# A four-layer image network on one core: the third layer's first pass issued in program order, the fourth layer's first inputs on three engines, and the first layer's gates placed between its transpositions

## The chip, the cores and the metric

The kernel runs on 1 core of one Trainium2 chip. The metric is the device time of one execution in microseconds. Engines are named as in the profile: PE (TensorE, matrix products and transpositions), PEld (its weight loads), DVE (VectorE), ACT (ScalarE), POOL (GpSimd) and SP (SyncE, which issues most DMAs). All data is 32-bit floating point.

## The reference

Eight images of 56 x 56 pixels and 192 channels go through four layers; each is a group normalization (32 groups), an operation, and a residual addition.

```python
x = x + L0(gn(x)); x = x + L1(gn(x)); x = x + L2(gn(x)); x = x + L3(gn(x))

# L0: gated Toeplitz operator, D1 = 576
p, q, v = silu(x @ p_w.T + p_b), silu(x @ q_w.T + q_b), silu(x @ v_w.T + v_b)
qv = q * v
o1 = toeplitz along w of qv with a1;  o2 = toeplitz along h of qv with a2
out = (p * (o1 + o2)) @ o_w.T + o_b

# L2: windowed attention over 8 x 8 windows, E = 384, S = 128
u, v, base = split(silu(x @ W_uv + b_uv))
lk = rope over the image(base * lk_g + lk_b)
lin_kv = sum over all tokens of lk^T (v / tokens)      # needs every token first
attn = relu(qq @ qk^T / 64 + bias) ** 2
out = u * (attn @ v + lq @ lin_kv) @ W_proj + b_proj

# L3: linear recurrences along four directions
h_t = h_{t-1} @ A + Bv * x_t;  y_t = Cv * h_t + (Dv + res) * x_t   # rows, columns, two diagonals
```

L1 (an attention over 3 x 3 patches) isn't touched.

## The kernel before, in words

The four layers run one after the other in one program. A framework places tiles in pools, inserts all semaphores, and orders the instructions of each engine by a plan made ahead of the run. Where a block is entered with `tc.manual_schedule(engines=...)`, the instructions of those engines keep the order in which the code states them, among those of that block; instructions of engines that aren't named, and of other blocks, may be placed by the plan wherever it thinks them ready.

**First layer (`layer0`, L136).** PE is in program order (L627); the other engines aren't. Each image goes through `NC = 5` chunks of channels, `c` = 0 to 4; chunks 0 to 3 have 128 channels, the last 64. For a chunk: `project` (L283) makes q and v from the normalized image in four steps `g` (PE products into accumulators from `banks()`, four in all, each of two PSUM banks; then two Silus on ACT into tiles `s`, of which there are four; then `multiply`, on DVE and POOL, writes the products into the one tile `qv`). Then `turn_both` (L342; `turn` for the last chunk) transposes `qv` in seven steps: 16 transpositions on PE into one accumulator, and two copies out of it, one on DVE and one on ACT (L357). Then `convolve` (L382) multiplies by the Toeplitz matrices. After chunks 1 and 3, `post` gates and projects back. The main loop (L634) interleaves lists of steps with `merge`: the transpositions of chunk `c` with the list `fill` (`post` or `post_tail` of an earlier chunk; `fill` is empty at c = 1 and c = 3 and at the very first chunk), then `project` of the next chunk with `beside` (statistics and normalization), then the convolutions; at `c == NC - 2` the steps of `project` and of `convolve` alternate.

**Third layer (`layer2`, L1241), first pass.** Its pools lie partly where the second layer's tiles lay. 52 iterations `n` (L1497) run over 50 groups of two tiles of 128 tokens, for pairs of images. In iteration `n`, PE multiplies the normalized tokens by `wvb` (`project`, L1412, accumulators `v`: three), `gates` (L1423) adds the bias on DVE (`sm`) and takes the Silu on ACT (`vb`), `keys` (L1433) stores v and builds the rotated key `l1` on POOL and DVE from the tables `ta`, `tb`, `tn`; two iterations later PE transposes the group's base (`turn`, into the one accumulator `t`) and adds `l1^T v` to `kv` (`sum_up`). `key_tables(c)` (L1380) loads six tiles' worth of the cosine and sine tables and multiplies the gains in, on DVE and POOL; it is called for c = 0 ahead of the loop and for the other four at the start of n = 1, 4, 7 and 10. `fetch` loads a chunk of the image (a chunk is seven tiles; SP queue, the first one ACT queue), `ready` normalizes it (ACT, and DVE for the second image) into window order. At given iterations `jobs` (L1490) run: the last statistics of the second layer (n = 3, 5, 7; two of them use the accumulator `t`), and loads of the second pass's weights, tables and bias. Only PE is in program order here (L1347). The second pass (L1527) puts DVE, ACT and POOL in program order too, SP not.

**Fourth layer (`layer3`, L1815).** PE, DVE, ACT and POOL are in program order. For each of four pairs of images, `inputs` (L1882) makes `u = scale * y + offset` in three parts `j`, one instruction of 128 x 3136 elements each; `inputs_diagonal` copies the diagonals on POOL; `step` (L1906) runs the recurrence, with the states in `ringv` and `ringh`. The first pair's `y` is loaded near the end of the third layer into tiles that are kept for it. At the start, inputs 0 and 1 are made on ACT and input 2 on POOL (L1993). The pool `l3u` (L1845) holds `us[0]` and then the two rings, in memory in which the second pass's tiles (`xa`, `xb`, `vt` and others) lay; a tile waits for what used its place.

Of the kernel before, what the change touches and what calls it, by code (L numbers as in the profile page):

```python
# [135 lines left out]
def layer0(cx, xin, xout, w, consts):  # L136
# [14 lines left out]
    with ExitStack() as es:  # L151
# [130 lines left out]

        def project(xn, c):  # L283

            n = 7 * H
            tail = c == NC - 1
            js = [2 * c] if tail else [2 * c, 2 * c + 1]

            def step(g):
                pss = [banks() for _ in js]  # L290
                for j, ps in zip(js, pss):
                    for h in range(2):
                        at = h * HQ + g * n
                        nc.tensor.matmul(  # L294
                            ps[:, h, 0:n], wqv[0][:, j, :], xn[0][:, at : at + n],
                            start=True, stop=False,
                        )
                for j, ps in zip(js, pss):
                    for h in range(2):
                        rows = slice(h * CB, (h + 1) * CB)  # L300
                        nc.tensor.matmul(  # L301
                            ps[:, h, 0:n], wqv[1][rows, j, :], xn[1][rows, g * n : (g + 1) * n],
                            start=False, stop=True,
                        )
                ts = []
                for i in range(2):
                    j, ps = js[0 if tail else i], pss[0 if tail else i]
                    rows = slice(i * DS, (i + 1) * DS) if tail else slice(0, 128)
                    t = cx.tile(wk, [128, 2, n], "s")[0 : DS if tail else 128]
                    nc.scalar.activation(t, ps[rows, :, 0:n], AF.Silu, bias=bqv[rows, j : j + 1])  # L310
                    ts.append(t)
                multiply(g, slice(0, DS if tail else 128), ts)

            return [lambda g=g: step(g) for g in range(4)]

        def multiply(g, rows, ts):

# [311 lines left out]
        merge(normalize(xn), [])  # L629
        for n in range(2):  # L630
            toeplitz(n)
        merge(project(xn, 0), [])
        fill, after, telling = [], None, []
        for b in range(B):  # L634
            more = b + 1 < B
            for c in range(NC):
                n = b * NS + 2 * c
                two = c < NC - 1
                turns = turn_both(n) if two else turn(n)
                merge(fill, turns)  # L640
                fill, beside = [], []
                if c == 0:
                    if after is not None:
                        image_dma(nc.sync, xout[b - 1], *after, store=True)
                        beside, telling = tell(b - 1, *after)
                    if more:
                        nxt = load_raw(b + 1)
                if c == 1:
                    acc = new_acc(b)
                    beside = [lambda f=f: f(bank) for f in telling]  # L650
                if c == 2 and more:
                    beside = normalize(nxt)

                if c % 2 == 0:
                    ot = cx.tile(cp, [120, 128, H] if two else [H, H, DS], "ot")
                ahead = project(xn, c + 1) if two else project(nxt, 0) if more else []
                convs = []
                for m in (n, n + 1) if two else (n,):
                    *some, last = convolve(m, ot)
                    convs += some + [lambda m=m, last=last: (last(), toeplitz(m + 2))]  # L660

                if c == NC - 2:
                    ahead = [f for pair in zip(ahead, convs[0:4]) for f in pair]
                    convs = convs[4:]
                merge(ahead, beside)
                for f in convs:
                    f()
                if c in (1, 3):
                    fill = post(c // 2, xn, ot, acc)
            fill, after = post_tail(xn, ot, acc), acc  # L670
            xn = nxt
# [569 lines left out]
def layer2(cx, xin, xout, w, consts):  # L1241
# [15 lines left out]
    with ExitStack() as es:  # L1257
# [90 lines left out]


        with ExitStack() as ps1:  # L1350
            def pool(name, bufs, **kw):
                return ps1.enter_context(tc.tile_pool(name=name, bufs=bufs, reuse_waits="tile", **kw))

# [23 lines left out]
            TW = 6  # L1377
            chunks = [(p, c) for p in range(NPAIR) for c in range(4)]

            def key_tables(c):  # L1380
                at = slice(c * TW, min((c + 1) * TW, NCH))
                n = at.stop - at.start
                a, b, t = ta[:, at], tb[:, at], tn[:, at]
                nc.sync.dma_start(a, consts["cos_rows"][:, at])
                nc.scalar.dma_start(b, consts["sin_rows"][:, at])
                g = [gk[:, i, :].unsqueeze(1).to_broadcast([128, n, S]) for i in range(4)]
                tmp = cx.tile(c1, [128, TW, S], "tmp")[:, 0:n]
                nc.vector.tensor_tensor(t, a, g[2], ALU.mult)
                nc.gpsimd.tensor_tensor(tmp, b, g[3], ALU.mult)
                nc.vector.tensor_tensor(a, a, g[0], ALU.mult)  # L1390
                nc.gpsimd.tensor_tensor(b, b, g[1], ALU.mult)
                nc.vector.tensor_tensor(t, t, tmp, ALU.add)
# [90 lines left out]

            ready(0)
            nc.scalar.dma_start(gk, w["lk_gb"].partition_broadcast(128))
            key_tables(0)
            fetch(1)


            jobs = [(3 + 2 * k, f) for k, f in enumerate(cx.late)]  # L1490
# [5 lines left out]
            kept = {}  # L1496
            for n in range(len(groups) + 2):  # L1497
                pvs = []
                if n in (1, 4, 7, 10):
                    key_tables((n + 2) // 3)  # L1500
                for at, job in jobs:
                    if at == n:
                        job()
                if n < len(groups):
                    p, g, ns = groups[n]
                    c = 4 * p + min(g // CW, 3)
                    if c + 1 not in xws:
                        fetch(c + 2)
                        ready(c + 1)
                    pvs = [cx.tile(psv, [128, 2, 512], "v") for _ in range(ns)]  # L1510
                    vb = cx.tile(wk, [128, 2, 2, E + S], "vb", bufs=4)
                    project(p, g, 0, pvs[0])
# [4 lines left out]
                if n < len(groups):  # L1517
                    for s in range(1, ns):
                        project(p, g + s, 0, pvs[s])
                    for s in range(ns):  # L1520
                        project(p, g + s, 1, pvs[s])
                        gates(g + s, pvs[s], vb, s)
                    kept[n] = (groups[n], keys(p, g, ns, vb), vb)
            nc.vector.tensor_scalar(kv, pkv, 1.0 / HW, None, ALU.mult)

# [289 lines left out]
def layer3(cx, xin, xout, w, consts):  # L1815
# [17 lines left out]
    with ExitStack() as es:  # L1833
# [9 lines left out]
        ys = [over.y, [cx.tile(cp, [128, HW], f"y1{j}") for j in range(2)]]  # L1843
        sps = [pool("l3s0")]
        up = pool("l3u")  # L1845
        us = [cx.tile(up, [128, 3, NS, NS], "u0")]
        rings = [cx.tile(up, [128, NR, 3, NS], f"ring{k}") for k in "hv"]
        sps.append(pool("l3s1", 2))
        yp = pool("l3y")
        ys[1].append(cx.tile(yp, [128, HW], "y12"))  # L1850
# [139 lines left out]
        loaded = {}  # L1990
        coefficients(0, over.nn[0])
        for j in range(3):
            inputs((nc.scalar, nc.scalar, nc.gpsimd)[j], 0, j)  # L1993
        inputs_diagonal(0)
        loaded[1] = load(1)
        plans = {g: prepare(g) for g in range(1, NG)}
# [96 lines left out]
```

## Time and profile before

| | us |
|---|---|
| median of 3 runs | 4215.12 (4203.36 to 4217.38) |
| profiled execution, its own time | 4220.94 |
| its span, first to last instruction | 4219.1 |
| first layer | 0 to about 2060 |
| second layer | to about 2717 |
| third layer, first pass | to 3177 |
| third layer, second pass | to 3857 |
| fourth layer | to the end |
| PE busy | 3948.1 (94% of the span) |
| DVE, ACT, POOL busy | 2336.7, 1785.5, 1512.0 |

The mean clock granted to PE is 0.978 of full speed. In the lines below, a line of the timeline has its start, its length, the engine, the line of the kernel, the operation, its output and inputs with their shapes, how many instructions are merged in it, and in brackets the idle time before it and what ended it. Durations of PE are modelled in part, since its instructions overlap. In the first layer an image takes about 249 us, as the distance of like stretches shows.

### The profile page before, as it was taken

How to read it: one execution, taken by the hardware profiler on the slowest of the kernel's cores; microseconds unless marked ns; L12 is line 12 of the kernel's file. 1: busy time of each engine (PE TensorE's matmuls, PEld its weight loads, DVE VectorE, ACT ScalarE, POOL GpSimd, SP SyncE). 2: the span in 40 equal slices, each digit the busy share in tenths (PEclk: the TensorE clock that was granted, in tenths of full speed). 3: DMA queues.
4: the chain of work that ended last, by engine and by line, in shares of the span. 5: the costliest groups of instructions: out<-in, count | busy, mean ns of one | idle time of the engine just before them, and what ended most of it. 6: DMA issues, size and time to landing. Idle time of an engine off the chain costs nothing.

```text
span 4219.1 us, 106491 instructions
## 1 busy us (share of the span) xinstructions
PE 3948.1 (94%) x46380; PEld 2547.7 (60%) x46380; DVE 2336.7 (55%) x3407; ACT 1785.5 (42%) x2022; POOL 1512.0 (36%) x1302
## 2 busy tenths in 40 slices
PE   6989999999999999999799999799998999998997
PEld 4666656666665666656466666444444555555997
DVE  5536565554656546554544444465656667664664
ACT  2434434334443434444233344233335555554564
POOL 3222232222322222242233333333334444443776
PEclk9999999999999999999899999899999999999999
DMA  6755242242524224242324444565538776663233
GB/s 145 141 107 146 62 116 66 77 97 62 146 62 113 58 70 115 62 105 66 92 66 110 105 101 106 138 185 186 167 130 192 174 171 150 159 144 104 81 110 94
DMA packets 382342, 483.54 MB, mean 115 GB/s; under 512 B 176084, under 2 KB 326724, under 8 KB 380484
## 3 DMA queue, kind: packets, MB, share of 16 engines
q1 hardware_dynamic: 375029, 467.19, 44.0%
q10 hardware_dynamic: 6847, 9.54, 0.8%
q8 instruction: 365, 5.98, 0.6%
q14 instruction: 101, 0.83, 0.1%
HBM read 320.90 MB, written 155.65 MB: 113 GB/s over the span
## 4 chain that ended last, share of the span: by engine, by line
PE 76%; DVE 7%; issue 6%; DMA 3%; POOL 3%; ACT 3%; SPq 1%; ACTq 0%; POOLq 0%; DVEq 0%
PE c L294 9%; PE h L1926 7%; PE v L1418 6%; PE c L395 6%; PE c L301 5%; PE c L481 5%; PE c L436 4%; PE c L948 4%; PE c L461 3%; PE y L983 3%; PE kv L1478 3%; PE c L443 3%; PE c L486 2%; DVE ol L357 2%; PE c L954 2%
## 5 line engine op out<-in xcount | busy, mean ns | idle before, releaser
L325 POOL TENSOR_TENSOR qv<-s,s 128x392 f32<-128x392 f32 (+3 forms) x320 | 567.2, 1793 | 1423.4 <-ACT s L310 1382.5
L310 ACT ACTIVATE s<-c,bqv 128x784 f32<-128x784 f32 (+1 forms) x320 | 278.5, 911 | 383.8 <-PE c L301 224.0
L294 PE MATMUL c<-xa,wqv 128*128 128x392 f32 x1152 | 432.3, 517 | 9.3 <-ACT or L357 6.5
L319 DVE TENSOR_TENSOR qv<-s,s 128x784 f32<-128x784 f32 (+1 forms) x160 | 190.5, 1190 | 267.0 <-ACT s L310 266.9
L357 ACT COPY or<-c 56x1024 f32<-56x1024 f32 x224 | 225.9, 1008 | 256.2 <-DVE ol L357 241.2
L294 PEld LDWEIGHTS c<-xa,wqv 128*128 128x128 f32 x1152 | 210.5, 194 | 177.3 <-issue 42.5
L395 PEld LDWEIGHTS c<-or,ol 120*64 120x64 f32 x9216 | 278.1, 138 | 59.4 <-issue 49.5
L395 PE MATMUL c<-or,ol 120*64 120x56 f32 x9216 | 288.7, 223 | 21.5 <-issue 8.4
L357 DVE COPY ol<-c 56x1024 f32<-56x1024 f32 x224 | 261.6, 1210 | 64.1 <-PE c L352 64.1
L450 ACT ACTIVATE s<-c,bp 128x448 f32<-128x448 f32 x224 | 129.9, 631 | 269.9 <-PE c L443 269.9
L301 PE MATMUL c<-xb,wqv 64*128 64x392 f32 x1152 | 232.9, 518 | 0.0
L1418 PE MATMUL v<-wvb,wa 128*128 128x512 f32 (+1 forms) x400 | 192.9, 615 | 28.7 <-ACT wa L1307 16.8
L1957 POOL TENSOR_TENSOR y<-y,s 128x448 f32<-128x448 f32 x168 | 185.0, 1101 | 91.9 <-ACT s L1936 88.6
L1926 PE MATMUL h<-ringv,am 128*64 128x57 f32 (+1 forms) x4400 | 192.4, 235 | 24.0 <-DVE ringv L1913 17.1
L481 PE MATMUL c<-po,wo 128*128 128x448 f32 x448 | 198.1, 564 | 10.8 <-DVE po L470 10.8
L1429 ACT ACTIVATE vb<-sm 128x1024 f32<-128x1024 f32 (+1 forms) x100 | 103.9, 1040 | 222.2 <-issue 195.6
L436 PE MATMUL c<-xa,wp 128*128 128x224 f32 x896 | 191.3, 356 | 3.6 <-issue 3.6
L1926 PE MATMUL h<-ringh,am 128*64 128x57 f32 (+1 forms) x4400 | 186.5, 232 | 8.4 <-DVE ringh L1932 7.8
L424 DVE TENSOR_TENSOR acca<-c,acca 128x392 f32<-128x392 f32 (+1 forms) x120 | 67.3, 588 | 222.0 <-PE c L486 204.8
L352 PE MATMUL c<-ident,qv 64*120 64x64 f32 x3584 | 143.2, 226 | 44.4 <-ACT or L357 38.9
L1926 PEld LDWEIGHTS h<-ringv,am 128*64 128x64 f32 x4400 | 168.1, 140 | 27.2 <-DVE ringv L1913 18.0
L948 PE MATMUL c<-wv,xc 128*126 128x192 f32 x896 | 175.6, 339 | 0.2 <-ACT v L958 0.2
(230 smaller groups left out, 7681.8 us busy)
## 6 DMA issues: line engine op xcount, KB each, us to landing
or<-tt SPq DMA_DIRECT2D x252, 196.0 KB
ol<-tt SPq DMA_DIRECT2D x252, 196.0 KB
vt<-v SPq DMA_DIRECT2D x56, 672.0 KB
v<-vb SPq DMA_DIRECT2D x96, 384.0 KB
x<-x SPq DMA_DIRECT2D x110, 168.0 KB
x<-x SPq DMA_DIRECT2D x110, 112.0 KB
bs<-bt SPq DMA_DIRECT2D x48, 256.0 KB
bs<-bs SPq DMA_DIRECT2D x54, 224.0 KB
```

What stands on the lines that cost most here:

```text
L294: nc.tensor.matmul(ps[:, h, 0:n], wqv[0][:, j, :], xn[0][:, at : at + n], start=True, stop=False,)
L301: nc.tensor.matmul(ps[:, h, 0:n], wqv[1][rows, j, :], xn[1][rows, g * n : (g + 1) * n], start=False, stop=True,)
L310: nc.scalar.activation(t, ps[rows, :, 0:n], AF.Silu, bias=bqv[rows, j : j + 1])
L319: nc.vector.tensor_tensor(sub(qv[rows, 7 * g :, 64 + H - 1 :], (HH * 120, 2), (120, 7), (-1, H)), *(t.rearrange("p u (h w) -> p u h w", w= ...
L325: eng.tensor_tensor(sub(qv[rows, w0:, H - 1 - 7 * g - HH * u :], (120, w1 - w0), (-1, 7)), *(t[:, u].rearrange("p (h w) -> p w h", w=H)[:, ...
L357: copy(dst[:, :, :, i0 : i0 + 8], view[rows])
L395: nc.tensor.matmul(ps[u * 64 : (u + 1) * 64, k, v * H : (v + 1) * H], left[:, d * H : d * H + 64], right[:, d * H : (d + 1) * H], start=Tr ...
L436: nc.tensor.matmul(out(u, h), wp[0][:, 2 * j + u, :], xn[0][:, at : at + n], start=(u == 0), stop=True, skip_group_check=True,)
L481: nc.tensor.matmul(pa, wo[:, 2 * j + u, 0:CA], pos[u], start=(u == 0), stop=(u == 1))
L948: nc.tensor.matmul(out(i, u), group(i, u), wv[0], start=(u == 0), stop=True, skip_group_check=True,)
L1418: nc.tensor.matmul(out, x[:, at : at + n], wt, start=(k == 0), stop=(k == 1), skip_group_check=True,)
L1926: nc.tensor.matmul(ps[sides[c], y], am[a][:, m * CB : (m + 1) * CB], old[:, x], start=(n < 2), stop=True, skip_group_check=True,)
```

## The change

First layer: `project` returns, for each step, a pair of functions: `gates` (products and Silus) and `products` (`multiply`). `whole` joins them again. In the main loop, `project` of the next chunk is called ahead of the transpositions; where `fill` is empty, the first two steps' `gates` are merged with the transpositions and their `products` follow them; the other steps run whole, as before. At `c == NC - 2` only as many steps of `convolve` alternate as steps of `project` are left.

Third layer, first pass: DVE, ACT, POOL and SP are put in program order. The table loads move out of `key_tables` into `fetch_tables`, both on SP: tables 0 ahead of the loop and ahead of `fetch(1)`, tables 1 after it, the others at n = 1, 4 and 7. `key_tables(0)` moves into the loop, and all its calls from an iteration's start to between `gates` and `keys`. The second chunk's `ready` and third chunk's `fetch` move from n = 0 to n = 2.

Fourth layer: the rings are placed ahead of `us[0]`, and the first pair's input 1 is made on DVE.

```diff
@@ project @@
-            def step(g):
+            state = {}
+
+            def gates(g):
                 pss = [banks() for _ in js]
...
-                multiply(g, slice(0, DS if tail else 128), ts)
-
-            return [lambda g=g: step(g) for g in range(4)]
+                state[g] = ts
+
+            def products(g):
+                multiply(g, slice(0, DS if tail else 128), state.pop(g))
+
+            return [(lambda g=g: gates(g), lambda g=g: products(g)) for g in range(4)]
@@ layer0, main loop @@
-        merge(project(xn, 0), [])
+        def whole(steps):
+            return [lambda f=f, h=h: (f(), h()) for f, h in steps]
+
+        merge(whole(project(xn, 0)), [])
...
-                merge(fill, turns)
+
+                ahead = project(xn, c + 1) if two else project(nxt, 0) if more else []
+                early = [] if fill else ahead[0:2]
+                merge(fill + [f for f, _ in early], turns)
+                for _, f in early:
+                    f()
+                ahead = whole(ahead[len(early) :])
...
-                ahead = project(xn, c + 1) if two else project(nxt, 0) if more else []
...
                 if c == NC - 2:
-                    ahead = [f for pair in zip(ahead, convs[0:4]) for f in pair]
-                    convs = convs[4:]
+                    k = len(ahead)
+                    ahead = [f for pair in zip(ahead, convs[0:k]) for f in pair]
+                    convs = convs[k:]
@@ layer2, first pass @@
         with ExitStack() as ps1:
+            ps1.enter_context(
+                tc.manual_schedule(engines={ET.DVE, ET.Activation, ET.Pool, ET.SP})
+            )
...
+            def fetch_tables(c):
+                at = slice(c * TW, min((c + 1) * TW, NCH))
+                nc.sync.dma_start(ta[:, at], consts["cos_rows"][:, at])
+                nc.sync.dma_start(tb[:, at], consts["sin_rows"][:, at])
+
             def key_tables(c):
...
-                nc.sync.dma_start(a, consts["cos_rows"][:, at])
-                nc.scalar.dma_start(b, consts["sin_rows"][:, at])
...
             nc.scalar.dma_start(gk, w["lk_gb"].partition_broadcast(128))
-            key_tables(0)
+            fetch_tables(0)
             fetch(1)
+            fetch_tables(1)
...
-                if n in (1, 4, 7, 10):
-                    key_tables((n + 2) // 3)
...
-                    if c + 1 not in xws:
+                    if n >= 2 and c + 1 not in xws:
                         fetch(c + 2)
                         ready(c + 1)
...
                         gates(g + s, pvs[s], vb, s)
+                    if n in (0, 1, 4, 7, 10):
+                        key_tables((n + 2) // 3)
+                        if n in (1, 4, 7):
+                            fetch_tables((n + 5) // 3)
                     kept[n] = (groups[n], keys(p, g, ns, vb), vb)
@@ layer3 @@
         up = pool("l3u")
+        rings = [cx.tile(up, [128, NR, 3, NS], f"ring{k}") for k in "hv"]
         us = [cx.tile(up, [128, 3, NS, NS], "u0")]
-        rings = [cx.tile(up, [128, NR, 3, NS], f"ring{k}") for k in "hv"]
...
-            inputs((nc.scalar, nc.scalar, nc.gpsimd)[j], 0, j)
+            inputs((nc.scalar, nc.vector, nc.gpsimd)[j], 0, j)
```

## The prediction

> **What bounds the kernel now.** I read the page first (busy shares, the chain that ended last), then busy time by stretches with the granted clock, then the timeline at every place where the TensorE (PE) stands still, then DVE alone inside the third layer's first pass. The page's chain, by engine:
>
> ```profile
> PE 76%; DVE 7%; issue 6%; DMA 3%; POOL 3%; ACT 3%; SPq 1%; ACTq 0%; POOLq 0%; DVEq 0%
> ```
>
> PE sets the pace, busy 3948.1 of 4219.1 us. So only time in which PE waits or runs at half clock can be won, and the change aims at three such places. By stretches (start:end, length, busy us of PE, PEld, DVE, ACT, POOL, granted clock, DMA share, GB/s):
>
> ```profile
> 616.30:619.60 3.30, 2.88 (x7) 1.60 (x6) 2.73 (x3) 2.93 (x4) 0.00 (x0) 0.51 0.94 276
> ...
> 2722.00:2734.20 12.20, 0.00 (x0) 0.00 (x0) 8.81 (x12) 0.81 (x2) 10.86 (x4) 0.51 0.85 231
> 2734.20:2753.00 18.80, 6.92 (x8) 2.35 (x8) 14.11 (x14) 6.02 (x8) 11.51 (x7) 0.50 0.64 148
> ...
> 3857.20:3870.10 12.90, 0.00 (x0) 0.00 (x0) 2.05 (x4) 6.53 (x3) 6.25 (x6) 0.69 0.65 184
> 3870.10:3882.70 12.60, 10.75 (x158) 10.06 (x160) 3.70 (x14) 5.89 (x2) 7.02 (x13) 0.50 0.73 213
> ```
>
> See: PE does nothing in the second and fourth line, 0.37 of its time in the third, and each pause is followed by half clock. The 15.2 us pause at 3177 between the third layer's passes is not touched.
>
> First layer, transpositions with nothing between them (timeline):
>
> ```profile
> 363.61 6.87 DVE L357 COPY ol<-c 56x1024 f32<-56x1024 f32 x6 [0.21 <-PE c L352]
> ...
> 367.05 0.69 PE L352 MATMUL c<-ident,qv 64*120 64x64 f32 x16 [0.45 <-ACT or L357]
> ...
> 368.18 2.90 PE L294 MATMUL c<-xa,wqv 128*128 128x392 f32 x8 [0.44 <-ACT or L357]
> ```
>
> See: PE needs 0.69 us for a step, the copies 6.87/6 = 1.15 us, so PE waits for a free accumulator. L352 has 44.4 us of such idle time in the page's groups.
>
> Third layer's start:
>
> ```profile
> 2734.20 2.07 PE L1418 MATMUL v<-wvb,wa 128*128 128x512 f32 x2 [16.78 <-ACT wa L1307]
> ...
> 2748.15 5.17 PE L1418 MATMUL v<-wvb,wa 128*128 128x512 f32 x6 [11.88 <-DVE wa L49]
> ```
>
> See: 16.78 us until ACT's input, 11.88 more until DVE's half of it, because DVE first worked through the five key tables (the chain of waits for 2700 to 2760 runs through `tb`, `tmp`, `tn`, `ta`). Inside the pass, DVE alone:
>
> ```profile
> 2785.68 2.36 DVE L1428 TENSOR_TENSOR sm<-v,bvb 128x1024 f32<-128x1024 f32 x2 [1.41 <-PE v L1418]
> 2788.18 0.16 DVE L1176 COPY gms<-t 128x3 f32<-128x3 f32 x1
> ...
> 2792.15 0.69 DVE L1455 TENSOR_TENSOR l<-l,l 128x512 f32<-128x512 f32 x1 [1.16 <-POOL l L1448]
> ```
>
> See: DVE runs in the program's order already, with 1.41 us of slack per group of 8.57 us, save that `gms` went ahead of `l`.
>
> Fourth layer's start:
>
> ```profile
> 3862.79 5.89 ACT L1875 ACTIVATE u<-y,co 128x3136 f32<-128x3136 f32 x2 [4.93 <-DMA x<-xb]
> ...
> 3870.11 1.49 PE L1926 MATMUL h<-ringv,am 128*64 128x114 f32 x20 [12.94 <-DVE ringv L1913]
> ```
>
> See: ACT waits for the last stores of layer 2 (`u` lies where their tiles lay), then makes two of three inputs one after the other.
>
> [...] Here ACT's copies wait for DVE's (241.2 us at L357), though they read other partitions. [...] The trace moves 231 GB/s at a share of 0.85 between 2722 and 2734, so order matters there.
>
> **Part 1, first layer.** Where no post-processing fills the transpositions (c = 1 and 3 of eight images, and c = 0 of the first: 17 places) two of four gate steps now stand before and among them, their products after. Nothing is added. A full gate step is 4.34 us of PE (340.51 to 344.85), its two Silus 1.72. Before: 6.4 us (transpositions and wait) + 2 x 4.35 = 15.1 until the third gate step. After, from zero: gates 0 to 4.35; steps 0 to 2 to 5.95 (the third waits for gate 0's Silu); gates 1 from 6.15 to 10.5; steps 3 to 6 to 12.9 (the last wait for its Silu); the third gate step wants the accumulators of steps 3 and 4, which copies at 1.1 us free at 13.4: it starts at 13.5. Gain 1.6. At c = 3 the gate step has one half, 2.2 us of PE, and the copies are the longer: 0.6 to 1.6, I take 1.2. Sum 8 x 1.6 + 8 x 1.2 + 2 = 24.4. Half-clock stretches right after the bare turns (616, 978, 1227: clock 0.51, 0.51, 0.50, about 1.6 us lost each) should go: 4. The products now start on POOL only when the transpositions have read `qv`. Cover: 16 us of convolutions follow the gates, and POOL needs 4 us per step, ending at about 28 as before. The four `s` buffers are held by the early gates: the third Silu comes (19) after POOL's first product (17). The statistics' two small matmuls at c = 1 now have one gate step between them, 4.35 against a DVE chain of 3.4: at most 1 us in all. Part 1: -28, bounds -10 and -42.
>
> **Part 2, third layer's first pass.** First, the start. DVE, ACT, POOL and SP keep program order, so the input comes before the tables, and the last three of five table pairs (384, 384 and 64 KB each table: 1.7 of 3.2 MB) are no longer fetched ahead of it. The input's target tile overlaps layer 1's last strips; their last update ends on DVE at 2719.5, the stores go out to about 2722 and land 2 us later (before, stores queued among the tables until 2726.8). ACT and DVE each need 0.73 to 0.76 for the first piece: PE starts at 2726.5 (2725 to 2731), and is not stopped for DVE. The third matmul comes at 2728.6 instead of 2748.15: -19.6. Second, what the order gives back. (a) At group 5 the statistics' `gms` copy frees the only `t` bank. In order it stands behind group 4's `l`, and behind the tables of groups 0, 1 and 4 (three operations of 0.96 us, L1388 to L1392: 2.9 us of DVE each). With DVE caught up, as in the trace of before, it comes at 2792.9, and the transposition that needs the bank at 2789.8: 3.1 us. But the three table sets put DVE back by 1.8 each (1.1 lies in its wait for the Silu), and groups 0 and 1 have no sums for PE to do, so PE gains another 1.5 on DVE there, while slack gives back about 1: late by 6, a wait of 9. I take 9, and 2 for the half clock after it. (b) Square root at group 7 behind group 6's Silu: 0.7. (c) DVE late at groups 2 to 4: 0.5. (d) `gbs` at group 18 waits for its six DMAs, about 3 us, inside the slack of 4 to 5 that three accumulators give; SP's 8 bias rows per group (about 0.5 us each) fit 8.57. Later groups run the order they had, cost 0. Queued behind these waits: on DVE `sm`, for which PE waits only two groups later; on SP the v and bt stores, with four and two buffers. Part 2: -19.6 + 12.2 = -7.4, bounds -17 (3.1 instead of 11) and +5 (start at 2731, more waits at 12 to 13).
>
> **Part 3, fourth layer.** Rings come before `u0`, which by the tile sizes moves `u0` 21.9 KB up, off the last strip's `xa` and `xb` onto `vt`, and rotation tiles that are free by about 3832. The second input goes to DVE: 1.91 to 3.19 us for 128x3136 (L49 `xa`), ACT's is 2.99, POOL's 2.96. If they start only after layer 2's last work: ACT 3857.9 to 3860.9, DVE 3859.9 to 3863.1, POOL 3859.2 to 3862.2; then 0.9 + 0.3 as now; PE at 3864.4, not 3870.1: -5.7. If they are moved ahead into layer 2's idle stretches (the coefficients already ran at 3469, amid layer 2), PE goes on at about 3857.5: -12.6, and most of the half clock of 3870.1 to 3882.7 (about 0.6 us for each of eight steps, 4.8) goes too: -17. The data is there (`y` loads were issued by 3841). I take -13.
>
> **Sum.** -28 - 7.4 - 13 = -48. The profiled execution took 4220.94, its span 4219.1; 4220.94 - 48 = 4173. The median of the runs is 5.8 below it: 4167.
>
> **Rivals.** R1, the ordered pass gives back all it wins and the inputs aren't moved ahead: -25 + 0 - 6: 4184. For it: the single `t` bank; against: only one such wait is certain. R2, no change: the gates among the transpositions only move the wait to the copies (DVE 8 us of 13 there), -6 with +5 in part 2 and -6 in part 3: about 4208. For it: DVE and ACT pace the steps now; against: PE's and the copies' row sums fit side by side. R3, slower: DVE's ordered chain (sm 2.36, wait 1.12, a2 1.83, wait 1.16, l 0.69 = 7.16 us, by group) becomes the pass's bound. It decides once in-order waits add more than the 1.41 us of slack; at 3.2 us more, 48 groups x 1.8 = +86, less 41 from parts 1 and 3: 4260. For it: in-order SP and ACT behind DMAs; against: the trace already shows this order in the later groups. R4, all cheap: -42 - 17 - 17: 4139.
>
> **How the numbers follow.** Forecast 0.51 (own range 4150 to 4183), R1 0.20, R4 0.12, R2 0.06, R3 0.11. A measurement of this kernel can tell about 0.3%, 12.6 us, from no change. Faster: 0.51 + 0.20 + 0.12 = 0.83; within: 0.06; slower: 0.11. The range 4142 to 4202 leaves out R3, most of R2 and the far end of R4, under 0.2.
>
> **What would show it.** Right: L352's idle time from 44 to under 15; L294 between L352's steps; first L1418 at 2726 less part 1's gain, no wait for DVE L49; a wait of PE at L1464 for `gms` of 3 to 10 us; no DMA wait at L1875, PE's pause before L1926 under 7 us. Wrong: L1418 waiting for DVE `sm` or `l` in every group, waits of 3 us and more at L1307 for `xa`, or copies on ACT that make gates wait for accumulators.

## The result and the profile after

The kernel after takes 4169.86 us (median of four runs, 4158.77 to 4177.58) beside 4216.25 for the kernel before: ratio 0.9894, interval 0.9877 to 0.9912, some 45 us less. Its profiled execution took 4164.87, its span is 4163.1. The forecast was 4167. The total came out and its terms did not:

| part, from the ends of PE's last product of each stage | before | after | difference | forecast |
|---|---|---|---|---|
| first layer | 2061.7 | 2012.0 | -49.7 | -28 |
| second layer (code not touched) | 655.7 | 651.1 | -4.6 | 0 |
| third layer, first pass | 459.8 | 467.9 | +8.1 | -7.4 |
| third layer, second pass (not touched) | 680.0 | 681.9 | +1.9 | 0 |
| fourth layer, to the end of the span | 361.9 | 350.2 | -11.7 | -13 |

The second layer, whose code is the same everywhere, takes 650.1 to 657.5 us in the thirteen profiled executions of all kernels here: a difference of a few us between two single executions can be chance.

The page of the kernel after: busy time by engine, the chain by engine and one line of the groups.

```profile
PE 3924.4 (94%) x46380; PEld 2539.9 (61%) x46380; DVE 2392.8 (57%) x3408; ACT 1777.8 (43%) x2021; POOL 1522.0 (37%) x1302
...
PE 76%; DVE 8%; issue 7%; ACT 3%; POOL 3%; DMA 2%; SPq 1%; ACTq 0%; DVEq 0%; POOLq 0%
...
L401 PE MATMUL c<-or,ol 120*64 120x56 f32 x9216 | 283.1, 223 | 8.6 <-DMA ol<-ed 5.1
```

The same group on the page of the kernel before, where it is L395:

```profile
L395 PE MATMUL c<-or,ol 120*64 120x56 f32 x9216 | 288.7, 223 | 21.5 <-issue 8.4
```

PE still sets the pace, and the chain has the shares it had. PE is busy for 23.7 us less than the 3948.1 of before, although it runs the same 46,380 products: the products themselves became shorter (the mean granted clock rose from 0.978 to 0.982). The convolution's group had 21.5 us of idle time before it and now has 8.6. The forecast had worked out only a small part of either.

Stretches of the kernel after (start:end, length, busy us of PE, PEld, DVE, ACT, POOL, granted clock, DMA share, GB/s): the place at c = 1 of one image, the convolution at c = 1 of another, and then the third layer's start, its sixth group, the fourth layer's start and the stretch behind it.

```profile
352.91:366.07 13.16, 12.27 (x147) 7.85 (x145) 5.79 (x6) 8.37 (x9) 0.71 (x1) 1.00 0.94 209
...
865.30:873.10 7.80, 7.80 (x258) 7.66 (x257) 7.05 (x11) 2.13 (x3) 3.34 (x3) 1.00 0.21 56
...
2663.10:2686.25 23.15, 0.00 (x1) 0.03 (x1) 5.68 (x10) 1.38 (x3) 0.00 (x0) 0.59 0.86 227
...
2731.40:2746.00 14.60, 5.96 (x14) 3.62 (x14) 8.95 (x12) 2.70 (x3) 3.99 (x3) 0.65 0.41 136
3812.90:3821.00 8.10, 0.00 (x0) 0.00 (x0) 6.03 (x5) 3.52 (x2) 6.29 (x6) 0.79 0.57 160
3821.00:3831.20 10.20, 8.34 (x118) 7.64 (x120) 2.85 (x11) 5.89 (x2) 6.93 (x13) 0.50 0.67 202
```

The first line is the place that was forecast to take 13.5 us, and it took 13.16, at full clock. Third line: PE is idle for 23.15 us at the third layer's start. Fourth line: a second pause, with half clock (0.65 in the stretch's mean), has come up inside the pass. Fifth line: the fourth layer's pause is 8.1 us where it was 12.9.

The place at c = 1 by PE's timeline:

```profile
357.17 1.58 PE L358 MATMUL c<-ident,qv 64*120 64x64 f32 x48
...
358.68 3.05 PE L297 MATMUL c<-xa,wqv 128*128 128x392 f32 x8
...
363.08 2.10 PE L358 MATMUL c<-ident,qv 64*120 64x64 f32 x64
...
366.07 2.90 PE L297 MATMUL c<-xa,wqv 128*128 128x392 f32 x8 [0.89 <-ACT or L363]
```

Gates (L297) stand between the transpositions (L358), and only the third gate step waits, 0.89 us, for the copies. In the whole layer L358 has 18.8 us of idle time ahead of it, where L352 had 44.4; nearly half of what is left is now a wait for a Silu (L313):

```profile
L358 PE MATMUL c<-ident,qv 64*120 64x64 f32 x3584 | 134.4, 223 | 18.8 <-ACT or L363 10.0 <-ACT s L313 8.6
```

The third layer's start, ACT's queue, the two input halves, and PE:

```profile
2675.83 0.34 ACTq L1283 DMA_DIRECT2D norm<-norm  x1
...
2683.20 1.08 ACTq L1385 DMA_DIRECT2D wvb<-in_l_W_vb  x2
...
2684.87 1.41 ACT L1322 ACTIVATE wa<-xa,norm 128x448 f32<-128x448 f32 x2 [29.10 <-DMA norm<-norm]
...
2685.75 1.39 DVE L49 TENSOR_SCALAR wa<-xa,norm 128x448 f32<-128x448 f32 x2 [17.44 <-DMA wvb<-in_l_W_vb]
...
2686.25 6.12 PE L1440 MATMUL v<-wvb,wa 128*128 128x512 f32 x8 [23.17 <-DMA wvb<-in_l_W_vb]
```

DVE no longer holds PE: it starts 0.9 us after ACT, and PE doesn't stop for it. What holds all three are loads: `norm` goes out between 2675.8 and 2682.7 and `wvb` at 2683.20, in that order behind the six image loads on ACT's queue. In the kernel before, `wvb` had been issued 6 us ahead of layer 1's end (2717.4):

```profile
2711.12 2.17 ACTq L1366 DMA_DIRECT2D wvb<-in_l_W_vb  x2
```

The sixth group of the pass, DVE and PE:

```profile
2727.78 2.28 DVE L1477 TENSOR_TENSOR l<-l,l 128x512 f32<-128x512 f32 x1 [1.16 <-POOL l L1470]
...
2739.24 0.69 DVE L1477 TENSOR_TENSOR l<-l,l 128x512 f32<-128x512 f32 x1
...
2739.86 0.15 DVE L1191 COPY gms<-t 128x3 f32<-128x3 f32 x1
...
2740.06 1.11 PE L1486 MATMUL t<-ident,vb 128*128 128x128 f32 x4 [8.63 <-DVE gms L1191]
```

`gms` stands behind a whole group of DVE's work and the tables, and the transposition that needs the one accumulator `t` waits 8.63 us: forecast 9.

The fourth layer's start:

```profile
3813.45 2.99 ACT L1900 ACTIVATE u<-y,co 128x3136 f32<-128x3136 f32 x1
...
3814.89 2.96 POOL L49 TENSOR_SCALAR u<-y,co 128x3136 f32<-128x3136 f32 x1
...
3815.48 4.02 DVE L49 TENSOR_SCALAR u<-y,co 128x3136 f32<-128x3136 f32 x1
...
3821.01 1.49 PE L1951 MATMUL h<-ringv,am 128*64 128x114 f32 x20 [8.14 <-DVE ringv L1938]
```

The wait for a DMA at `u` is gone. The inputs start after layer 2's last work, none was moved ahead.

### The profile page after: what moved, and what is told of

The parts are those of the page before. It is cut to its first block, busy times and chain, and to the rows that moved or that the text cites. A ratio compares the mean times of both kernels' runs of the same rounds, so it can differ in the third digit from the quotient of the medians.

```text
span 4163.1 us, 106509 instructions
## 1 busy us (share of the span) xinstructions
PE 3924.4 (94%) x46380; PEld 2539.9 (61%) x46380; DVE 2392.8 (57%) x3408; ACT 1777.8 (43%) x2021; POOL 1522.0 (37%) x1302
## 3 DMA queue, kind: packets, MB, share of 16 engines
q8 instruction: 365, 5.98, 0.6%
## 4 chain that ended last, share of the span: by engine, by line
PE 76%; DVE 8%; issue 7%; ACT 3%; POOL 3%; DMA 2%; SPq 1%; ACTq 0%; DVEq 0%; POOLq 0%
PE c L297 8%; PE h L1951 7%; PE v L1440 6%; PE c L401 6%; PE c L487 5%; PE c L442 4%; PE c L304 4%; PE c L963 4%; PE c L467 3%; PE y L998 3%; PE kv L1500 3%; PE c L449 3%; PE c L492 2%; PE c L969 2%; PE c L1661 2%
## 5 line engine op out<-in xcount | busy, mean ns | idle before, releaser
L331 POOL TENSOR_TENSOR qv<-s,s 128x392 f32<-128x392 f32 (+3 forms) x320 | 579.8, 1838 | 1360.3 <-ACT s L313 1128.3
L297 PE MATMUL c<-xa,wqv 128*128 128x392 f32 x1152 | 426.5, 511 | 19.8 <-ACT or L363 12.1
L313 ACT ACTIVATE s<-c,bqv 128x784 f32<-128x784 f32 (+1 forms) x320 | 278.4, 910 | 355.0 <-PE c L304 201.4
L325 DVE TENSOR_TENSOR qv<-s,s 128x784 f32<-128x784 f32 (+1 forms) x160 | 248.0, 1562 | 150.2 <-ACT s L313 150.1
L297 PEld LDWEIGHTS c<-xa,wqv 128*128 128x128 f32 x1152 | 206.4, 191 | 182.9 <-issue 32.4
L430 DVE TENSOR_TENSOR acca<-c,acca 128x392 f32<-128x392 f32 (+1 forms) x120 | 67.2, 586 | 221.4 <-PE c L492 204.5
L1469 POOL TENSOR_TENSOR l<-vb,ta 128x512 f32<-128x512 f32 (+1 forms) x52 | 75.2, 1446 | 273.1 <-ACT vb L1451 268.5
```

The costliest lines, as they stand in the source:

```text
L297: nc.tensor.matmul(ps[:, h, 0:n], wqv[0][:, j, :], xn[0][:, at : at + n], start=True, stop=False,)
L325: nc.vector.tensor_tensor(sub(qv[rows, 7 * g :, 64 + H - 1 :], (HH * 120, 2), (120, 7), (-1, H)), *(t.rearrange("p u (h w) -> p u h w", w= ...
L331: eng.tensor_tensor(sub(qv[rows, w0:, H - 1 - 7 * g - HH * u :], (120, w1 - w0), (-1, 7)), *(t[:, u].rearrange("p (h w) -> p w h", w=H)[:, ...
```

## The experiments

The theory after this reading: part 1 gives some 50, part 2 costs some 10 because loads stand in a row on ACT's queue and `t` is freed late, part 3 gives 5 to 6. The rivals: the forecast's own terms (-28, -7.4, -13), with chance between two single executions for the rest.

| run | us, with its interval, against the kernel before |
|---|---|
| the change | -44.7 (-51.9 to -37.1) |
| the change, measured again | -43.9 (-49.3 to -38.0) |
| part 1 alone | -49.4 (-54.5 to -43.9) |
| part 1 at c = 1 alone | -24.9 (-29.9 to -19.8) |
| stores moved, no early gates | -16.1 (-21.1 to -10.6) |
| part 2 alone | +10.6 (+7.6 to +13.5) |
| part 3 alone | -3.4 (-7.2 to 0) |
| part 3, rings alone | -9.7 (-14.3 to -5.1) |
| parts 1 and 3 | -60.0 (-66.8 to -53.2) |
| the change, weights first | -61.3 (-67.2 to -55.4) |
| weights first, statistics later | -57.8 (-63.7 to -51.4) |
| the pass mended | -69.3 (-75.6 to -63.4) |

Each is its ratio less one, times the median of before on its chip (4216.25, 4225.42, 4216.66 or 4224.73).

### Each part alone

Part 1 alone: the first layer's edit on the kernel before.

> The kernel before with the first layer's edit alone. By the prediction: -28 us (bounds -10 and -42), made of 16 places at 1.6 and 1.2. By the two traces: the places give 1.8 and 1.7 each, about -28 with them alone; the rest of the -49.7 in the first layer would be half-clock windows (4 fewer of 3.4 us, about 8) and stalls of PE that no record explains (10.8 us in the profiled run of before, 1.1 in that of after). If these belong to the change, the run is 42 to 50 us faster; if they are chance of the one profiled execution, 28 to 35. The third layer starts as before (two waits, 16.8 and 11.9) and its first pass takes about 460 us.

-49.4 us; the first layer ends at 2014.4. In the seven profiled executions with the edit it ends at 2010.0 to 2015.2, in the four without any edit there at 2056.4 to 2066.7. The gain belongs to the change, and the forecast's -28 is out.

Part 2 alone: the pass in order, with its table loads.

> The kernel before with the third layer's first pass in program order alone. By the prediction: -7.4 us (PE starts 9 us after layer 1's last product and is not held for DVE: -19.6; 12.2 given back). By the traces: +5 to +10, because the weights wvb and the statistics norm stand behind six image loads on ACT's queue (one start wait of 23 us instead of 16.8 and 11.9), and the turn at the sixth group waits 8 to 9 us for the only bank t, with 10 us of half clock after it. Rival: the place of layer 2's tiles or the state of the DMA lanes differs without the other edits, then the start wait is not 22 to 24.

+10.6 us. Start of the pass, from its timeline:

```profile
2735.41 1.24 ACTq L1370 DMA_DIRECT2D wvb<-in_l_W_vb  x2
...
2738.61 6.63 PE L1425 MATMUL v<-wvb,wa 128*128 128x512 f32 x8 [21.78 <-DMA wvb<-in_l_W_vb]
```

The wait is 21.78 us and that for `gms` 8.65: the two waits of the kernel after, without the other parts. So part 2 is a loss by itself.

Part 3 alone: rings ahead of `u0`, input 1 on DVE.

> The kernel before with the fourth layer's edits alone (rings ahead of u0, first input 1 on DVE). By the prediction: -13 us as a mean of -5.7 (inputs after layer 2's last work) and -17 (moved ahead). By the trace of after: the inputs are not moved ahead, the pause is 8 instead of 13 us: -5 to -6, and the further 6 us in the fourth layer come from a pause of 4.1 us late in it (near 4107 in before) that no part of the change touches. If that pause is chance, this run is 5 to 7 us faster; if it hangs on where u0 and the rings lie, 11 to 13.

-3.4 us. The pause before the first step is 8.09 us; the later pause, 4.12 us at 4107 in the kernel before, is there too, with 3.26. Such waits of PE for the next pair's `u` come up none, one or two times in an execution, with the edits (none in the first profile of after, one of 2.90 in the second) and without (one of 4.12 in before; 3.51 and 3.31 in part 1 alone). They are not the change's: it gives 5 to 6 us and not 12. Over all profiled executions, the fourth layer takes 358.4 to 364.1 us in the five without this edit (mean 361.4) and 350.2 to 358.3 in the eight with the rings moved (355.2), 6 us less.

### The whole change again, and the parts that are worth it

> The kernel after once more, as the reference of the other runs of this set on one chip. The three parts alone gave -49.4, +10.6 and -3.4 us: if they only add, -42 (4183 where before takes 4225). If they help or hinder each other, more than 6 us off that.

-43.9 us: the parts add up (-49.4 + 10.6 - 3.4 = -42.2).

Parts 1 and 3, with the first pass of before:

> The kernel before with the first and fourth layer's edits, the third layer's first pass as before: what the change gives without its second part. By the parts alone (-49.4, -3.4 to -9.7): -53 to -59; the second part alone cost 10.6, and the whole change gave -44. If the ordered pass only costs because it stands behind the other parts' edits, this is no faster than the whole change.

-60.0 us: without its second part the change gives 16 more, with intervals that don't touch.

### Third layer: the order of the loads, and the bank

Weights first:

```diff
-            raw, xws = {0: load(xp, 0, 0, 2, nc.scalar)}, {}
-            fetch_norms(0, nc.scalar)
             wvb = [cx.tile(c1, [128, E + S], f"wvb{k}") for k in range(2)]
...
             nc.scalar.dma_start(bvb, w["b_vb"].partition_broadcast(128))
+            fetch_norms(0, nc.scalar)
+            raw, xws = {0: load(xp, 0, 0, 2, nc.scalar)}, {}
```

> The kernel after, with the loads of wvb, bvb and the four of norm issued on ACT's queue ahead of the first six image loads instead of behind them. If their place in the queue is what starts PE late: PE waits 12 to 14 us instead of 23, ACT's first input ends near 12 us after layer 1's last product, and the kernel is about 10 us faster than after (54 below before). If their data had to wait for layer 1's memory in any case, or the image loads are late by the same amount: no change. A loss (a few us) if the weights' memory is freed later than the image's, so that the image loads queue behind them.

-61.3 us, more than the 54 expected. The pass is 8.1 us shorter (459.8); the rest of the 17 us between the two ratios lies in stages that this edit doesn't touch, and isn't explained. ACT's queue and PE:

```profile
2655.19 0.82 ACTq L1383 DMA_DIRECT2D wvb<-in_l_W_vb  x2
...
2672.89 2.07 PE L1440 MATMUL v<-wvb,wa 128*128 128x512 f32 x2 [10.92 <-ACT wa L1322]
...
2679.52 5.05 PE L1440 MATMUL v<-wvb,wa 128*128 128x512 f32 x6 [4.56 <-DVE wa L49]
```

`wvb` now goes out 6.8 us ahead of layer 1's end (2662.0), and PE starts after 10.92 us, near the 9.1 of the forecast. What then stops it is DVE's half, 4.56 us, waiting for the second image's loads.

Weights first, and the last statistics called behind the turn and the sums:

```diff
-            jobs = [(3 + 2 * k, f) for k, f in enumerate(cx.late)]
+            lates = {3 + 2 * k: f for k, f in enumerate(cx.late)}
...
                     sum_up(n - 2, ns0, 2 if g0 < NCH - 1 else 1, l1, vb0)
+                if n in lates:
+                    lates[n]()
```

> The kernel after with the weights and norm ahead of the image loads, and the last statistics of layer 2 called after an iteration's turn and sums instead of ahead of its products, so that the turn after them comes a whole group later. If the turn's wait for gms (7.0 us with the weights first, 8.6 in after) comes from the order of DVE and the one bank t: the wait falls under 1.5 us, the 7 to 10 us of half clock behind it go, and the pass is 9 to 11 us shorter than with the weights first (449 to 451 instead of 459.8). If the group of DVE work behind it is the real limit, the wait only moves to a product (for sm or l) or to the square root's turn, and the pass stays within 3 us of 459.8.

The pass takes 454.9 us: 4.9 shorter, where 9 to 11 were expected; the time (-57.8) can't be told from the run above. The wait for `gms` is gone. From PE's timeline, what came instead:

```profile
2726.39 2.72 PE L1170 MATMUL t<-mean,gmat 128*128 128x1 f32 x14 [2.27 <-ACT bt L1490]
```

The statistics' product now follows the turn in the same bank and waits for ACT's copy out of it. The bank was the limit, and it still costs 2.27 us.

All mended: the statistics behind the second tile's first products, and the second chunk and its tables fetched behind the first group's stores.

```diff
             fetch_tables(0)
-            fetch(1)
-            fetch_tables(1)
...
                     for s in range(1, ns):
                         project(p, g + s, 0, pvs[s])
+                    if n in lates:
+                        lates[n]()
...
                     kept[n] = (groups[n], keys(p, g, ns, vb), vb)
+                    if n == 0:
+                        fetch_tables(1)
+                        fetch(1)
```

> The kernel after with three mends in the third layer's first pass: weights and norm ahead of the image loads; the last statistics called behind the second tile's first products (so that their product doesn't wait 2.3 us for ACT's copy out of the bank t); the second chunk's image loads and tables fetched behind the first group's stores instead of beside the first chunk's loads. If the 5.2 us in which PE waits for DVE's input come from the second image's loads sharing the queues and lanes with the next chunk: that wait falls under 2 us, the statistics' wait under 1, and the pass takes 446 to 449 us instead of 454.9: about 7 us faster than without the last two mends, 20 faster than after (4197 to 4200 where before takes 4217 would be after; this 4153). If the second image's loads are late by themselves (layer 1's stores before them): the wait stays at 5 and only 1 to 2 us are won. If the late fetch starves the fourth group, a new wait of some us near the third group takes its place.

-69.3 us, the pass 445.7. PE's waits in its first 60 us:

```profile
2680.02 5.79 PE L1440 MATMUL v<-wvb,wa 128*128 128x512 f32 x8 [10.66 <-ACT wa L1322]
...
2704.81 0.66 PE L1486 MATMUL t<-ident,vb 128*128 128x128 f32 x4 [0.75 <-ACT bt L1490]
2706.62 2.85 PE L1500 MATMUL kv<-vb,l 128*128 128x384 f32 x8 [1.16 <-DVE l L1477]
...
2729.63 1.72 PE L1170 MATMUL t<-mean,gmat 128*128 128x1 f32 x14 [0.56 <-ACT bt L1490]
```

One wait of 10.66 us is left, then none over 1.2 in the whole pass. PE no longer stops for DVE's half, which cost 4.56 us with the weights first. So the second image's loads were late because the next chunk's stood beside them. This version is the fastest of all: 25 us faster than the change itself, by the two ratios.

### Fourth layer: which of the two edits

> The kernel before with only the rings ahead of u0; inputs 0 and 1 stay on ACT. By the prediction half of part 3's gain is DVE taking the second input. By the traces ACT would end its two inputs 5.9 us after its start and DVE ended its one 4.0 us after a start that was 2 us later: the pause is 8 us here too, and the kernel is as fast as with both edits (-3.4 us, or 5 to 6 by its pause and half clock). If DVE's input matters, the pause is 10 us or more.

ACT's two inputs and PE's first step in the run with the rings alone:

```profile
3846.40 5.88 ACT L1875 ACTIVATE u<-y,co 128x3136 f32<-128x3136 f32 x2
...
3853.72 1.49 PE L1926 MATMUL h<-ringv,am 128*64 128x114 f32 x20 [7.89 <-DVE ringv L1913]
```

The pause is 7.89 us. The place of the rings gives all of it. DVE gives nothing: it starts 2.0 us after ACT and needs 4.02 us, so it ends with ACT's second input. The times of this run and of both edits (-9.7 and -3.4) have intervals that overlap from -7.2 to -5.1, where the traces' 5 to 6 lie.

### First layer: where fifty come from

The early gates at c = 1 alone (`early = ahead[0:2] if c == 1 else []`):

> The kernel before with the first layer's edit at c = 1 alone (8 of 17 places). By the prediction's sizes: -13 for the waits, -2 to -3 for half clock: -15. By the traces: the stretch of c = 1 became 3.9 us shorter per image and that of c = 3 only 2.0, with the half-clock windows and the stalls without a releaser (11 to 15 us in three executions without the edit, 1 in three with it) following the bare transpositions of c = 1: about -31, the stalls under 4 us and the half clock in the first layer 40 us or less instead of 56 to 61. If the stalls and windows hang on c = 3, they stay and the run is 13 to 16 us faster.

-24.9 us, half of part 1; so the other places, c = 3 above all, give the other half. The stalls of PE that have no releaser (idle times over 0.3 us) come to 11.0 to 18.2 us per first layer in the four executions without an edit there, more than the 9 to 15 that the next expectation counts. Here they fell to 1.3, as expected of c = 1. The half clock did not: 51.2 us, where it is 47.8 to 61.4 in the four executions without an edit there and 23.8 to 37.5 in the seven with the whole one. As far as one execution tells, that goes with c = 3. The reading of -31 was too much for c = 1.

Many of the stalls sit in the convolution that follows. In the kernel before, its stretch in one image and PE's timeline there:

```profile
886.10:897.80 11.70, 8.27 (x259) 7.96 (x257) 5.41 (x6) 3.40 (x4) 2.80 (x3) 1.00 0.54 111
```
```profile
886.09 3.88 PE L395 MATMUL c<-or,ol 120*64 120x56 f32 x125
891.06 4.06 PE L395 MATMUL c<-or,ol 120*64 120x56 f32 x129 [1.09 <-issue]
897.46 0.32 PE L395 MATMUL c<-or,ol 120*64 120x56 f32 x2 [2.34 <-issue]
```

11.7 us for 256 products that take 7.7 to 7.8 in the kernel after (the second stretch shown above), at 111 GB/s against 56. The change had also moved something that no line of its diff names: with the gates gone ahead, the second statistics product of the previous image comes right before the convolution, its two small stores six microseconds into it (871.42 and 871.81 in the convolution from 865.30), and of the next Toeplitz loads on SP's queue all but the first pair go out behind them, from 872.38 on. In the kernel before, the stores go out at 886.19 and 886.58 and the loads from 888.20 on. That alone, on the kernel before:

```diff
+                if c == 1 and beside:
+                    convs.insert(1, beside.pop())
                 merge(ahead, beside)
```

> The kernel before, only with the last step of the previous image's statistics (its matrix product, square root and the two small stores) called behind the first step of the convolution at c = 1 instead of ahead of it. SP then issues one pair of the next Toeplitz loads, the two stores, and the other loads behind them, as in the kernel after; the transpositions stay as before. Without the edit this convolution took 7.7 to 11.7 us at a DMA share of 0.41 to 0.54; with it 7.7 us in nearly all images at 0.21 to 0.23, and the stalls without a releaser were gone. If the loads beside the convolution stall PE: the convolutions at c = 1 take 7.7 to 8 us, the stalls fall from 9 to 15 us to under 4, the kernel is about 10 us faster than before, and some 10 us of what the first part gave are a side effect of the stores' place. If the early gates themselves remove the stalls: they stay, and the kernel is within 4 us of before.

-16.1 us. The convolution at c = 1 of the image that took 11.7, with the statistics' product of 1.05 us now inside it:

```profile
881.60:890.40 8.80, 8.80 (x267) 8.66 (x265) 5.79 (x9) 3.66 (x5) 3.70 (x3) 1.00 0.53 53
```

It takes 8.8 us in six images and 8.9 in the seventh that has statistics, without a stall; 6.5 us of stalls, where under 4 were expected, are left at other places. These seven convolutions take 65.1 us together in the kernel before and, without the statistics' product, about 55 here: 10 of the 16 us. The first layer ends at 2046.9, 14 us ahead of the mean of the four without an edit. So some 10 to 16 of part 1's 49 us are not the gates' own, if the two gains add.

Whether the place of the stores and loads does it or that of the statistics' own work, no run separates. It is not the rate of the loads alone: 111 GB/s against 53 and 56 speaks for it, but another convolution of the kernel before moved 210 GB/s without a stall, and the first of the two stalls above (889.97 to 891.06) lies where hardly anything moved:

```profile
852.87:860.55 7.68, 7.68 (x260) 7.62 (x260) 5.79 (x6) 2.13 (x3) 3.77 (x3) 1.00 0.79 210
```
```profile
886.00:891.00 5.00, 3.97 (x127) 3.75 (x125) 2.53 (x4) 2.59 (x3) 2.40 (x3) 1.00 0.21 18
```

Where in PE's instructions the second stall falls, the last section shows.

## Why the prediction was right in sum and wrong in its parts

**Part 1, -28 against -49.4.** The mechanism held, and its two place terms came out nearly: 13.16 us for the place against 13.5; at c = 3, from the convolution's end to the first product of `post`, 25.04 us before (471.68 to 496.72) and 23.35 after (459.71 to 483.06), 1.7 against 1.2. With 1.9 (15.1 less 13.16) and 1.7 eight times each, 29 where the forecast's sum had 22.4. Two terms were mis-sized. The half clock was put at 4 to 5 us for three stretches; it fell from 56.3 to 34.1 us. PE was busy in 48.0 and 32.6 of these, and about half of that is lost time, an estimate from the granted 0.50 (in the fourth layer of the kernel before, the same 20 products took 1.49 us at 0.50, from 3870.11, and 0.83 at full clock, from 3882.79): 8 between these two executions, 10 between the means of the four without the edit and the seven with it. And the statistics at c = 1 were booked as a cost of up to 1. That cost came and was larger (idle time before L98 went from 0.8 to 4.6), but moving the step, with the two stores that it issues, gave 10 to 16. The forecast counted PE's work around it and left out the two DMAs and what stands behind them, and it has no term for PE's stalls without a releaser. Together 29 + 10 + 10 to 16 - 4 = 45 to 51. Of the forecast's own signs, L352's idle time missed its mark: 18.8 where under 15 was to show.

**Part 2, -7.4 against +10.6.** The step that failed is the start, "PE starts at 2726.5": 9 us after layer 1's end. It was worked out from the image loads and DVE's tables, and the weights and `norm`, which the plan used to issue ahead of them, were taken as there. In the program's order they come last on ACT's queue. The third product came 24.9 us after layer 1's end instead of 11.2 (the kernel before: 30.8): -5.9 in place of -19.6. The give-back of 12.2 was right: 8.63 for `gms` (9), 0.79 for the square root (0.7), 1.45 and 0.60 more (0.5), and 3.4 us more at half clock, half of it lost: 13.2. That makes +7.3, beside 8.1 between the two profiles and 10.6 in the runs. R3 did not happen: no group waits for `sm`.

**Part 3, -13 against -3 to -10.** Of the two cases the first came, inputs not moved ahead, put at -5.7: the pause went from 12.94 to 8.14 us, 4.8. The number taken, -13, lies between the two cases (-5.7 and -17) and is near neither; the -11.7 between the two profiles is this gain and a chance pause. The pause before the first step, 8.14 us, missed its mark of under 7. DVE's input, taken at 1.91 to 3.19 us, took 4.02, with GpSimd's own of 2.96 beside it (last section).

**The sum.** -28, -7.4 and -13 give -48; -49.4, +10.6 and -3.4 give -42, the change itself -44 to -45. Part 1 was forecast 21 us too small, part 2 was 18 and part 3 8 to 10 too good. That errors of 21 and of 26 to 28 us cancel is luck: the total of 4167 beside 4169.86 says nothing for the three mechanisms. R1 (0 and -6 for parts 2 and 3) was nearer in these two and had part 1 as small.

## What to carry to other kernels

Putting a block into program order fixes the order of its DMAs as well: before doing so, write the loads that everything waits for first in each queue, then those for the next step, and look at what a plan had moved ahead without being told (here the weights' place alone took the wait at the start from 23.17 to 10.92 us). When a step moves, follow the DMAs that it issues: two stores of 1.5 KB together changed when other loads went out, and moving the step that issues them was worth a third to a half of what the transpositions' places gave (10 to 16 us beside 29). A total that comes out right says nothing of its terms: here the parts run alone showed that one of them gave away 11 to 16 us of what the others won.

## What the runs showed of the hardware

**Most of PE's stalls without a releaser come at one number in 256.** The idle times without a releaser are not scattered. Number PE's records in order of time from 0: products, weight loads, and the waits that its sequencer records between them. In the four executions without part 1's edit the first layer has 50 such stalls over 0.3 us. In 34 of them the instruction that comes late has a number that leaves 193 when divided by 256, among them the second of the two shown above (number 17601), with one at the same number in each of the three other executions (2.22, 0.40 and 1.92 us). The profile has a queue for instructions alone; its line on the page of the kernel before:

```profile
q8 instruction: 365, 5.98, 0.6%
```

5.98 MB in 365 packets are 16.4 KB each, and PE's 93,458 records are 365 times 256 and 18 more: as the counts go, a packet for every 256 records. When the first layer ended, 163 packets had landed and 162.8 times 256 of PE's records had started. The trace has each packet of this queue. All the stalls at this number, 55 in the first layers of the thirteen executions, took 0.3 to 3.3 us and end 1.2 to 1.8 us after one of these packets has landed; for the stall up to 897.46 it landed at 896.10. That fits a wait of PE for the instructions in the packet; no run isolates it.

Most often PE goes past this number without a stall, and where it stalls, the DMA engines are mostly busy. Of the places with this number in these first layers where the 256 records before took at most 4.6 us, apart from the stall itself (the convolution's 512 take 7.7), none of 65 had a stall of over 0.3 us where the DMA share in the 4 us before was under 0.2, 10 of 205 between 0.2 and 0.6, 11 of 88 between 0.6 and 0.8, and 28 of 65 above. That goes together; no run isolates it. The 16 other stalls all lie in the convolutions at c = 1, none is left in any run in which the statistics' step stands later, and what they wait for isn't explained.

**DVE's scale and offset takes longer beside GpSimd.** Two of the eight such instructions of 128 x 3136 elements in the kernel before:

```profile
46.28 1.91 DVE L49 TENSOR_SCALAR xa<-xa,rstd,nbias 128x3136 f32<-128x3136 f32 x1
```
```profile
709.49 3.86 POOL L325 TENSOR_TENSOR qv<-s,s 128x392 f32<-128x392 f32 x2 [2.12 <-ACT s L310]
...
711.84 3.15 DVE L49 TENSOR_SCALAR xa<-xa,rstd,nbias 128x3136 f32<-128x3136 f32 x1
```

With nothing on GpSimd it takes 1.91 us. In the seven others a GpSimd instruction is under way when DVE's starts; they take 3.14 to 3.19 us and end about 1.65 us after GpSimd's has ended (713.35 and 714.99 here). The new input in the fourth layer takes 4.02 us and again ends 1.65 us after GpSimd's (3817.85 and 3819.50). The 1.91 to 3.19 us of the forecast were thus not a spread: one ran alone, the others beside GpSimd. What ties DVE's end to GpSimd's, no run shows.

**Half clock without a long pause.** In the kernel before, the half clock that the prediction shows from 616.30 sets in at the end of a bare place at c = 1 whose waits are all under 1 us. Another such place has the same waits and kept full clock:

```profile
860.48:866.91 6.43, 4.16 (x116) 3.62 (x112) 5.70 (x6) 4.94 (x5) 0.00 (x0) 1.00 0.91 245
610.30:616.74 6.44, 4.20 (x117) 3.62 (x113) 5.71 (x6) 4.94 (x5) 0.00 (x0) 0.95 0.91 240
```

So with PE busy for 4.2 of 6.4 us half clock can come, and doesn't always. The filled place shown above, busy for 12.27 of 13.16, kept full clock.
